# Two iterations a unit in place of three in the attention stream of a perceiver kernel

## Chip, core and metric

The kernel runs as one program on one core of a Trainium2 chip. The metric is the time of an execution on the device in microseconds (us), median over several runs. The engines are named as in the profile: PE is TensorE (matmuls), PEld its weight loads, DVE VectorE, ACT ScalarE, POOL GpSimd, and SP the queue that issues nearly all DMAs. Each engine takes its instructions in the order in which the program lists them.

## The reference

The model is a perceiver of two layers: cross attention, self attention and a feed-forward block, twice, each added to the stream `x`. Most of the time goes into the two cross attentions, of 64 queries per batch entry against a context of 1601 rows, for 32 entries and 16 heads of 16 values:

```python
x   : (32, 64, 256)      ctx : (32, 1601, 256)
# layer 0 (layer 1 is alike, with a mask over the context and no output projection)
q = split_heads(layernorm(x) @ wq + bq)
k = split_heads(ctx @ wk + bk)
v = split_heads(ctx @ wv + bv)
p = softmax(q @ k.T [+ mask], axis=-1)
x = x + concat(p @ v) @ wo + bo
```

The self attentions and feed-forward blocks of layer 0 are computed beside this stream, the last two blocks of layer 1 after it.

## The kernel before

`stream()` computes both cross attentions. Its work is cut into 256 **units** `u`: 2 layers x 32 batch entries x 4 groups of four heads. For a unit the kernel does the following, all in an order that is written out by hand (the framework places the waits, not the order):

- `maxima(u)` (L1225): scores with queries on the partitions, for the row maxima alone. Four steps of four matmuls `sp` (L1236, on 64x64 corners of the array) and two DVE reductions `mx` (L1241) each; the fourth step also makes the negated maximum `neg`, `mm`. A fifth step turns it with four small matmuls `rp` (L1256, one output row each) and copies it on ACT into a row of the query tile `qst` (two copies, L1261), so that the score matmuls that follow subtract it.
- `probabilities(u, j)` (L1267) for j = 0 to 6: scores with the context on the partitions, matmuls `tp` (L1277, whole array; 8 for each j, 4 for j = 6) into one of two PSUM buffers of `ps_t`, and one ACT exponential `e` (L1282) into one of three buffers of the pool `pt`.
- `weighted(u, j, e)` (L1285): the sums of values weighted by `e`, matmuls `acc` (L1292, on 32-column strips of the array).

Keys and values are made 1.8 batch entries ahead by the generator `projections()` (L1069). It alternates between a **keys call** (12 matmuls `kp`, L1089, and two DVE copies `kr` with the bias, L1095) and a **values call** (12 matmuls `vp`, L1117, and one ACT copy `v` out of PSUM, L1122, right behind them). A pair of context blocks needs one of each, and a unit needs 3.25 calls. `keys_values(target, slack)` (L1300) makes as many as its target asks for.

Each pair of blocks also needs casts on ACT, which are held as generators in the list `cuts` and moved on by `tick()` (L1005): `chi` (L986; POOL makes `clo` from it) splits a loaded block for the matmuls, and `ks` (L1039 and, when POOL has taken the difference, L1046) splits keys into three parts, which a DMA then stores to `kd` (L1049). A tick runs at most `left = 2` such pieces of work, and issues the loads `raw` (L974) that were listed one tick earlier (`loads`, then `due`). `fetch(u + 2)` (L1187) reads a unit's keys back with eight DMAs on SP (L1203 and L1208, a ninth with the mask in layer 1) into one of three `kst` buffers; the buffer is free when the last `tp` matmuls of unit u - 1 have read it.

PSUM buffers of `ps_m` (five, handed out in turn by `bank`) hold `sp`, `kp`, `vp`, `rp` and what the side work needs. The **side work** (queries, self attention and feed-forward of layer 0, the ends of finished rows) is moved on by `group_step()` and `end_step()`, one step at a call; its tiles lie in the pool `bg` by tags.

Before, a unit has three iterations. On PE their order is:

```
i=0: sp sp | acc(u-1: 5,6)        | tp 0,1 | side work | projections | tp 2
i=1: sp sp | acc(u: 0,1,2)        | tp 3,4 | side work | projections |
i=2:         acc(u: 3,4) | rp(u+1)| tp 5,6 | side work | projections | side work
```

with a tick before each of the three projections.

Of the kernel before, what the change touches and what calls it, by code (L numbers as in the profile page):

```python
# [20 lines left out]
F32 = mybir.dt.float32  # L21
# [9 lines left out]
P = 128  # L31
# [15 lines left out]
NH = 32  # L47
# [14 lines left out]
class Kernel:  # L62
# [215 lines left out]
    def stream_setup(self, wp, bg, bank):  # L278

        nc, ins = self.nc, self.ins  # L280
# [36 lines left out]
        yield  # L317
        self.eye = wp.tile([P, NQ], BF16, tag="eye", name="eye")
        nc.vector.tensor_tensor(self.eye, self.ident[:, :64], self.ident[:, 64:], ALU.add)
        tri = bg.tile([P, P], F32, tag="oT", name="tri")  # L320
        nc.gpsimd.memset(tri, 1.0)
        nc.gpsimd.affine_select(
            out=tri, in_=tri, pattern=[[-1, P]], compare_op=ALU.is_gt, fill=0.0,
# [185 lines left out]
    def stream(self):  # L509
        nc, tc, ins = self.nc, self.tc, self.ins  # L510
        with ExitStack() as ctx:
# [6 lines left out]
            kq = pool("kq")  # L518
            kp_ = pool("kst")
            vp_ = pool("v")  # L520
            pt = pool("pt", 3)
            small = pool("s", 4)
            work = pool("w", 2)
            bg = pool("bg", 1)
# [281 lines left out]
            def self0(g):  # L806
                xT = yield from normed(g, "sa0")
                rp = bank(f"sa0_rp{g}")
                for cc in range(2):
                    nc.tensor.matmul(  # L810
                        rp[: 3 * NH, : 2 * P], self.basT[:, cc, : 3 * NH], xT[:, cc, :],
                        start=(cc == 0), stop=(cc == 1),
                    )
                rT = bg.tile([3 * NH, 2 * P], F32, tag="oT", name=f"sa0_rT{g}")
                nc.scalar.copy(rT, rp[: 3 * NH, : 2 * P])
                yield
                qp = bank(f"sa0_qp{g}").rearrange("p (c n) -> p c n", c=2)
                for c in range(2):
                    nc.tensor.matmul(
                        qp[:, c, :], self.wT[:NH, c * P : (c + 1) * P], rT[:NH],  # L820
                        start=True, stop=True,
                    )
                qT = bg.tile([P, 2, 2 * P], F32, tag="qf", name=f"sa0_qT{g}")
                nc.scalar.mul(qT, qp, 0.25)
                yield
                kp = bank(f"sa0_kp{g}").rearrange("p (c n) -> p c n", c=2)
                for c in range(2):
                    nc.tensor.matmul(
                        kp[:, c, :], self.wT[NH : 2 * NH, c * P : (c + 1) * P], rT[NH : 2 * NH],
                        start=True, stop=True,  # L830
                    )
                kT = bg.tile([P, 2, 2 * P], F32, tag="kT", name=f"sa0_kT{g}")
                nc.scalar.copy(kT, kp)
                yield
                values(g, "sa0", [rT[2 * NH : 3 * NH]], [self.wT[2 * NH : 3 * NH]], None)
                yield

                def out(t, oT):
                    rp = bank(f"sa0_ro{g}_{t}")
                    for c in range(2):  # L840
                        nc.tensor.matmul(
                            rp[:NH, :P], self.basT[:, c, 3 * NH :], oT[:, c, :],
                            start=(c == 0), stop=(c == 1),
                        )
                    ro = bg.tile([NH, P], F32, tag="ro", name=f"sa0_rs{g}_{t}")
                    nc.scalar.copy(ro, rp[:NH, :P])
                    yield
                    ao = bank(f"sa0_ao{g}_{t}")
                    nc.tensor.matmul(ao[:, :D], ro, self.woT, start=True, stop=True)
                    x = self.X[:, 2 * g + t, :]  # L850
                    nc.vector.tensor_tensor(x, x, ao[:, :D], ALU.add)
                    yield

                yield from attention(g, "sa0", qT, kT, None, out)

            def ffn0(g):
# [12 lines left out]

                def wide(tag, dt=F32):  # L870

                    home = dict(dg="oT", row="ro").get(tag, f"ff_{tag}")
                    return bg.tile([P, 2, NQ], dt, tag=home, name=f"ff0_{tag}{g}")


# [113 lines left out]
                )  # L989
                return hi, lo  # L990

            kds, vs, ksts, cuts, loads, due = {}, {}, {}, [], [], []

            vring = [
                [
# [9 lines left out]
            def tick(b=-1):  # L1005


                if b < 0:
                    due[:], rest = loads[:], due[:]
                    del loads[:]  # L1010
                    for one in rest:
                        one()
                left = 2
                for one in list(cuts):
                    work = one[1] == "work"
                    if one[0] > b and work:
                        if left == 0:
                            continue
                        left -= 1
                    while True:  # L1020
                        one[1] = next(one[2], None)
                        if one[1] is None:
                            cuts.remove(one)
                        if one[1] is None or one[0] > b:
                            break
# [6 lines left out]
            def parted(i, x, quick):  # L1032

                m = 2 * width(i)
                ks = work.tile([P, 3, 2, KG], BF16, tag="ks", name=f"ks{i}", bufs=3)
                eng = nc.vector if quick else nc.gpsimd
                yield "work"
                x = x[:, :, :m]
                nc.scalar.copy(ks[:, 0, :, :m], x)  # L1039
                eng.tensor_tensor(x, x, ks[:, 0, :, :m], ALU.subtract)  # L1040
                eng.tensor_tensor(ks[:, 2, :, :m], x, upper(x), ALU.subtract)  # L1041
                if not quick:

                    yield "wait"
                    yield "work"
                nc.scalar.copy(ks[:, 1, :, :m], upper(x))  # L1046
                yield "store"
                for b, k0, n, o in spans(i):
                    nc.sync.dma_start(  # L1049
                        kds[b].rearrange("s (c q) (h n) -> (q h) s c n", c=2, h=4)[  # L1050
                            :, :, :, k0 : k0 + n
                        ],
                        ks[:, :, :, o : o + n],
                    )
# [10 lines left out]
            keyed = {}  # L1065

            NEVER = 2 * NB

            def projections():  # L1069

# [32 lines left out]
                def values(i):  # L1103
# [8 lines left out]
                    for i1 in range(2):  # L1112
                        o = slice(i1 * w_, (i1 + 1) * w_)
                        j = 0
                        for cc in range(2):
                            for x, w in ((hi, 0), (hi, 1), (lo, 0)):
# [2 lines left out]
                                    start=(j == 0), stop=(j == 5),  # L1119
                                )  # L1120
                                j += 1
                    nc.scalar.copy(  # L1122
                        v[:w_, :, :, :16], vp[:w_].rearrange("p c (h d) -> p c h d", d=16)
                    )
                    return 12 * D

                def fetched(i):
# [19 lines left out]

                def halved(i):
                    if raws[i] is None:
                        left = due + loads  # L1150
                        del due[:], loads[:]
                        for one in left:
                            one()
                    parts[i] = split(i)
                    return
                    yield
# [30 lines left out]
            def fetch(u):  # L1187

                b, q4 = divmod(u, 4)
                while keyed.get(b, 0) < NCH:  # L1190
                    made[0] += next(proj)
                tick(b)
                k = kring[u % 3]
                if u == 2:
# [197 lines left out]
            def banks_made(n):  # L1392
                for _ in range(n):
                    made[0] += next(proj)
                    tick()

            banks_made(1)
# [11 lines left out]
            fetch(1)  # L1409
            banks_made(3)  # L1410
            LEAD = 1.8
            for i, _ in enumerate(maxima(0)):
                if i < 4:
                    banks_made(1)
            groups.append((15, self.stream_setup(wp, bg, bank)))
            late = []
            for u in range(NU):
# [14 lines left out]
                    groups.append((u + 15, queries(*divmod((u + 15) // 16, NG))))  # L1432
                if u + 2 < NU and u + 2 not in ksts:
                    fetch(u + 2)
                nat = maxima(u + 1) if u + 1 < NU else iter(())

                for i, js in enumerate(((0, 1, 2), (3, 4), (5, 6))):
                    for _ in range((2, 2, 0)[i]):
                        next(nat, None)
                    for done in late:  # L1440
                        weighted(*done)
                        if done[1] == 6 and done[0] % 8 == 7:
                            n, t = divmod(done[0] // 8, NT)
                            ends.append((n, t, finish(n, t)))
                            next(ends[-1][2])
                    if i == 2:
                        next(nat, None)
                    late = [(u, j, probabilities(u, j)) for j in js[:2]]
                    banks[0] = 0
                    group_step()  # L1450
                    end_step()
                    tick()
                    keys_values(LEAD + (3 * u + i + 1) / 12.0, 0.15)
                    late += [(u, j, probabilities(u, j)) for j in js[2:]]
                    if i == 2:
                        group_step()
                        if u % 2:
                            end_step()
                for _ in nat:
                    pass  # L1460
            for done in late:
                weighted(*done)
            ends.append((1, NT - 1, finish(1, NT - 1)))
# [973 lines left out]
```

## Time and profile before

| what | value |
|---|---|
| time, median of 3 runs | 3648.9 us (3648.11 to 3666.66) |
| the profiled execution, and its span | 3643.7 us, 3642.0 us |
| granted TensorE clock over the span | 0.956 (0.98 to 1.00 from 300 to 3050 us, 0.83 after 3150 us) |
| last `acc` of the stream | at about 3108 us |
| from 300 to 3000 us: PE, PEld, DVE, ACT, POOL busy | 2591, 2171, 1735, 1885, 1468 us of 2700 |
| one exponential `e` (L1282) | 565 ns mean, 1792 of them |
| one cast `chi` (L986), `ks` (L1039, L1046) | 609, 606, 610 ns |
| one copy `v` out of PSUM (L1122) | 588 ns, 416 of them |
| one copy of the maxima (L1261) | 364 ns, two a unit |
| one bias copy `kr` on DVE (L1095) | 470 ns, two a keys call |
| one `clo` on POOL (L987) | 1246 ns |
| DMAs that read keys back (L1203, L1208) | 1024 of 208 KB and 1024 of 104 KB |
| DMA engines busy in the stream | 0.73 to 0.85 of the time, 200 to 240 GB/s |

Busy times are unions of what one engine has in flight. A matmul's recorded duration (195 to 305 ns) is its latency; matmuls follow one another much closer than that, so a PE that is busy all the time may still be slowed at the places where its starts lie further apart. For those, starts in the timeline are read.

### The profile page before, as it was taken

The numbers are of one execution on the slowest core, as the hardware profiler recorded it, in microseconds if no ns is written. First come the engines' busy times: TensorE is split into PE (matmuls) and PEld (weight loads), VectorE is DVE, ScalarE is ACT, GpSimd is POOL, SyncE is SP. The second block draws the span as 40 slices with busy tenths as digits, with TensorE's granted clock in tenths as the row PEclk, the third lists the DMA queues.
The fourth block names the chain that finished last, engine by engine and source line by source line (L and its number), as shares of the span: only waits on it lengthen the run. The fifth ranks groups of instructions, "written<-read, shape, count | busy, mean of one in ns | idle before, by whom it ended". The sixth has DMA issues, their size and how long they took to land. (4 is left out here: it accounts for less than half of the span.)

```text
span 3642.0 us, 148306 instructions
## 1 busy us (share of the span) xinstructions
PE 3316.4 (91%) x62993; PEld 2707.7 (74%) x63007; DVE 2417.2 (66%) x6166; ACT 2367.8 (65%) x4656; POOL 1792.4 (49%) x2109
## 2 busy tenths in 40 slices
PE   6899999999999999999999999999999998775698
PEld 5678887878778787778887778878778786332467
DVE  4556665666666566566667666656666566789879
ACT  3677766767667776667676777677667676154562
POOL 2455454555545554545555655556456563003246
PEclk8999999999999999999999999999999999887699
DMA  7888777777777777777787777777778887100000
GB/s 179 214 231 230 203 191 213 205 207 201 204 193 205 211 208 214 200 198 200 204 216 210 199 209 197 195 210 202 206 206 232 231 241 194 60 1 1 1 5 20
DMA packets 616920, 651.22 MB, mean 179 GB/s; under 512 B 127216, under 2 KB 581444, under 8 KB 599684
## 3 DMA queue, kind: packets, MB, share of 16 engines
q1 hardware_dynamic: 616256, 641.73, 64.3%
q8 instruction: 495, 8.11, 1.0%
q14 instruction: 169, 1.38, 0.1%
HBM read 468.30 MB, written 171.11 MB: 176 GB/s over the span
## 5 line engine op out<-in xcount | busy, mean ns | idle before, releaser
L1241 DVE TENSOR_REDUCE mx<-sp 128x1 f32<-128x400 f32 (+1 forms) x2048 | 1031.8, 565 | 324.5 <-PE sp L1236 323.9
L1282 ACT ACTIVATE e<-tp 128x512 f32<-128x512 f32 (+1 forms) x1792 | 931.7, 565 | 465.4 <-PE tp L1277 456.4
L987 POOL TENSOR_TENSOR clo<-raw,chi 128x512 fp32r<-128x512 f32 (+1 forms) x408 | 508.3, 1246 | 558.7 <-ACT chi L986 552.4
L1040 POOL TENSOR_TENSOR kr<-kr,ks 128x512 f32<-128x512 f32 (+1 forms) x406 | 459.4, 1132 | 608.7 <-ACT ks L1039 570.9
L1095 DVE TENSOR_SCALAR kr<-kp,bk 128x256 f32<-128x256 f32 (+1 forms) x832 | 356.3, 470 | 542.1 <-PE kp L1089 441.0
L1277 PE MATMUL tp<-qst,kst 128*128 128x64 bf16 (+1 forms) x13312 | 579.9, 195 | 15.0 <-ACT e L1282 13.1
L1292 PEld LDWEIGHTS acc<-e,v 128*17 128x17 f32 x26624 | 395.6, 98 | 213.2 <-issue 139.7
L1292 PE MATMUL acc<-e,v 128*17 128x64 f32 x26624 | 540.9, 222 | 13.2 <-ACT e L1282 10.5
L1277 PEld LDWEIGHTS <-kst 128*128 128x128 bf16 (+1 forms) x13312 | 462.2, 100 | 114.8 <-issue 22.0
L1117 PE MATMUL vp<-w_hi,chi 128*128 128x256 f32 (+1 forms) x1664 | 508.0, 305 | 15.7 <-DVE w_hi L222 12.4
L1117 PE MATMUL vp<-w_lo,chi 128*128 128x256 f32 (+1 forms) x1664 | 473.3, 284 | 0.4 <-DVE w_lo L223 0.3
L1117 PE MATMUL vp<-w_hi,clo 128*128 128x256 f32 (+1 forms) x1664 | 473.6, 285 | 0.0
L1041 POOL TENSOR_TENSOR ks<-kr 128x512 bf16<-128x512 f32 (+1 forms) x406 | 413.5, 1018 | 31.9
L1236 PE MATMUL sp<-kst,qst 64*64 64x400 bf16 (+1 forms) x4096 | 319.2, 349 | 92.0 <-DMA kst<-kd 41.2
L1089 PE MATMUL kp<-chi,w_hi 128*128 128x256 f32 (+1 forms) x1664 | 371.3, 305 | 14.4 <-DVE w_hi L222 6.2
L1122 ACT COPY v<-vp 128x512 f32<-128x512 f32 (+1 forms) x416 | 244.8, 588 | 184.9 <-PE vp L1117 181.7
L1089 PE MATMUL kp<-clo,w_hi 128*128 128x256 f32 (+1 forms) x1664 | 339.0, 285 | 15.3 <-POOL clo L987 14.5
L1117 PEld LDWEIGHTS vp<-w_hi,chi 128*128 128x128 f32 (+1 forms) x1664 | 313.9, 189 | 33.5 <-issue 9.5
L1089 PE MATMUL kp<-chi,w_lo 128*128 128x256 f32 (+1 forms) x1664 | 337.4, 285 | 0.0
L986 ACT CAST chi<-raw 128x512 fp32r<-128x512 f32 (+1 forms) x410 | 249.8, 609 | 105.6 <-DMA raw<-in_ctx_dram 105.4
L1117 PEld LDWEIGHTS vp<-w_lo,chi 128*128 128x128 f32 (+1 forms) x1664 | 314.6, 189 | 1.7 <-DVE w_lo L223 0.9
L1117 PEld LDWEIGHTS vp<-w_hi,clo 128*128 128x128 f32 (+1 forms) x1664 | 313.7, 189 | 0.0
(721 smaller groups left out, 5113.0 us busy)
## 6 DMA issues: line engine op xcount, KB each, us to landing
kst<-kd SPq DMA_DIRECT2D x1024, 208.0 KB
kd<-ks SPq DMA_DIRECT2D x384, 384.0 KB
kst<-kd SPq DMA_DIRECT2D x1024, 104.0 KB
raw<-in_ctx_dram SPq DMA_DIRECT2D x379, 256.0 KB
qst<-xa_qd SPq DMA_DIRECT2D x192, 64.0 KB
kd<-ks SPq DMA_DIRECT2D x64, 108.0 KB
xa_qd<-xa_qs SPq DMA_DIRECT2D x16, 384.0 KB
raw<-in_ctx_dram SPq DMA_DIRECT2D x62, 72.0 KB
```

The lines of the kernel that those rows point to most:

```text
L986: nc.scalar.copy(hi[:, :, :n], raw[:, :, :n])
L987: (nc.vector if i < 2 else nc.gpsimd).tensor_tensor(lo[:, :, :n], raw[:, :, :n], hi[:, :, :n].bitcast(F32), ALU.subtract)
L1040: eng.tensor_tensor(x, x, ks[:, 0, :, :m], ALU.subtract)
L1041: eng.tensor_tensor(ks[:, 2, :, :m], x, upper(x), ALU.subtract)
L1089: nc.tensor.matmul(kp[:, oc, :m], wk[w][:, cc, oc * P : (oc + 1) * P], x[:, cc, :m], start=(j == 0), stop=(j == 5),)
L1095: nc.vector.tensor_scalar(r[:, oc, :m], kp[:, oc, :m], self.bk[n][:, oc : oc + 1], None, ALU.add,)
L1117: nc.tensor.matmul(vp[:w_, i1, :], x[:, cc, o], wv[w][:, cc, :], start=(j == 0), stop=(j == 5),)
L1236: nc.tensor.matmul(sp[a][64 * j : 64 * j + 64, :n], q[r, h0 + 2 * j + a, tok], k[r, 2 * a + j, k0 : k0 + n], start=True, stop=True,)
L1241: nc.vector.tensor_reduce(mx[:, a, g : g + 1], sp[a][:, :n], AX.X, ALU.max)
L1277: nc.tensor.matmul(sp[:m, c, h, :], k[:, 2 * (h % 2) + h // 2, k0 : k0 + m], q[:, h0 + h, tok], start=True, stop=True,)
L1282: nc.scalar.activation(e[:m, :two], sp[:m, :two], AF.Exp)
L1292: nc.tensor.matmul(acc[32 * h : 32 * h + 17, slot, :], vs[b, c][:m, 4 * q4 + h, :], e[:m, c - 2 * i, h, :], start=(c == 0), stop=(c == NCH ...
```

## The change

A unit has two iterations. The order on PE becomes:

```
i=0: sp sp | acc(u-1: 4,5,6) | rp(u) | side work | projections | tp 0,1 | side work | projections | tp 2,3
i=1: sp sp | acc(u: 0,1,2,3) | side work | tp 4,5 | projections | tp 6 | side work
```

A tick stands behind each of the two `acc`, and runs up to three pieces of work. The fifth step of `maxima(u)` (`rp` and the two copies) moves from the end of unit u - 1 to the first iteration of unit u, behind the tick. A values call's copy `v` is listed in `held` and given to ACT later, by `copied()`: in front of the next projections and at the end of an iteration. Loads are issued by the first tick behind their listing (`due` is gone); the second cast of `ks` comes one tick behind the first, not two. `banks`, which limits the projections, no longer counts the side work. `end_step` is called four times a unit, not three or four. `pt` has four buffers, for which five tiles of `bg` take other tags.

```diff
-        tri = bg.tile([P, P], F32, tag="oT", name="tri")
+        tri = bg.tile([P, P], F32, tag="e", name="tri")
...
-            pt = pool("pt", 3)
+            pt = pool("pt", 4)
...
-                rT = bg.tile([3 * NH, 2 * P], F32, tag="oT", name=f"sa0_rT{g}")
+                rT = bg.tile([3 * NH, 2 * P], F32, tag="kz", name=f"sa0_rT{g}")
...
-                    ro = bg.tile([NH, P], F32, tag="ro", name=f"sa0_rs{g}_{t}")
+                    ro = bg.tile([NH, P], F32, tag="xT", name=f"sa0_rs{g}_{t}")
...
-                    home = dict(dg="oT", row="ro").get(tag, f"ff_{tag}")
+                    home = dict(dg="kz", row="kT").get(tag, f"ff_{tag}")
...
                 if b < 0:
-                    due[:], rest = loads[:], due[:]
+                    now = loads[:]
                     del loads[:]
-                    for one in rest:
+                    for one in now:
                         one()
-                left = 2
+                left = 3
...
                 eng.tensor_tensor(ks[:, 2, :, :m], x, upper(x), ALU.subtract)
-                if not quick:
-
-                    yield "wait"
-                    yield "work"
+                yield "work"
                 nc.scalar.copy(ks[:, 1, :, :m], upper(x))
...
+            def copied():
+
+                for one in held:
+                    one()
+                del held[:]
...
-                    nc.scalar.copy(
+
+                    held.append(lambda: nc.scalar.copy(
                         v[:w_, :, :, :16], vp[:w_].rearrange("p c (h d) -> p c h d", d=16)
-                    )
+                    ))
...
-                nat = maxima(u + 1) if u + 1 < NU else iter(())
-
-                for i, js in enumerate(((0, 1, 2), (3, 4), (5, 6))):
-                    for _ in range((2, 2, 0)[i]):
+                nat, own = maxima(u + 1) if u + 1 < NU else iter(()), nat
+
+                def some(*js):
+                    late.extend((u, j, probabilities(u, j)) for j in js)
+
+                def behind():
+
+                    group_step()
+                    end_step()
+
+                def made_up_to(part):
+                    copied()
+                    banks[0] = 0
+                    keys_values(LEAD + (u + part) / 4.0, 0.15)
+
+
+                for i in range(2):
+                    for _ in range(2):
                         next(nat, None)
                     for done in late:
                         weighted(*done)
...
-                    if i == 2:
-                        next(nat, None)
-                    late = [(u, j, probabilities(u, j)) for j in js[:2]]
-                    banks[0] = 0
-                    group_step()
-                    end_step()
+                    late = []
                     tick()
-                    keys_values(LEAD + (3 * u + i + 1) / 12.0, 0.15)
-                    late += [(u, j, probabilities(u, j)) for j in js[2:]]
-                    if i == 2:
-                        group_step()
-                        if u % 2:
-                            end_step()
-                for _ in nat:
-                    pass
+                    if i == 0:
+                        next(own)
+                        behind()
+                        made_up_to(1 / 3.25)
+                        some(0, 1)
+                        behind()
+                        made_up_to(2 / 3.25)
+                        some(2, 3)
+                    else:
+                        behind()
+                        some(4, 5)
+                        made_up_to(1.0)
+                        some(6)
+                        behind()
+                    copied()
```

The start of the program calls `copied()` behind each projection call too, so nothing changes there but the ticks.

## Prediction

> **What bounds the kernel now.** I read the page first: engine totals, then the slices.
>
> ```profile
> PE 3316.4 (91%) x62993; PEld 2707.7 (74%) x63007; DVE 2417.2 (66%) x6166; ACT 2367.8 (65%) x4656; POOL 1792.4 (49%) x2109
> PE   6899999999999999999999999999999998775698
> ```
>
> PE is above nine tenths from slice 3 to 34, the stream (to about 3108 us). What follows it, some 530 us, the change does not touch. Next, sums over single units late in the stream, where there is no side work (columns: stretch, its length, then busy us of PE, PEld, DVE, ACT, POOL, clock, DMA share, GB/s):
>
> ```profile
> 2914.60:2923.80 9.20, 9.20 (x213) 7.90 (x212) 5.32 (x13) 7.86 (x17) 5.57 (x6) 1.00 0.65 168
> 2933.00:2943.70 10.70, 10.70 (x229) 9.36 (x229) 6.19 (x15) 7.49 (x16) 5.97 (x6) 1.00 0.88 244
> ```
>
> Three projection calls make a unit of 9.2 us, four one of 10.7, and PE is busy for all of both, ACT for 70 to 85%. So a unit is as long as PE's own order, and ACT has 1.3 to 3.2 us to spare. Then the waits from 300 to 3000 us, 228 units (total us, times, longest):
>
> ```profile
> PE sp L1236 <- DMA kst<-kd: 13.9, 14, 3.3
> PE tp L1277 <- ACT e L1282: 8.5, 8, 1.7
> PE acc L1292 <- ACT e L1282: 3.9, 3, 3.0
> PE sp L1236 <- ACT v L1122: 1.1, 4, 0.4
> ...
> ACT e L1282 <- PE tp L1277: 394.1, 431, 5.2
> ACT chi L986 <- DMA raw<-in_ctx_dram: 70.4, 29, 5.5
> ...
> SPq L1203 <- PE tp L1277: 190.1, 109, 7.1
> ```
>
> PE hardly waits for ACT; ACT waits for PE. What the order of PE can save must therefore lie between matmuls. The timeline of the unit at 2933 us shows it (start, length, engine, line):
>
> ```profile
> 2933.00 0.54 PE L1236 MATMUL sp<-kst,qst 64*64 64x401 bf16 x8
> 2933.10 0.58 ACT L1122 COPY v<-vp 72x512 f32<-72x512 f32 x1
> ...
> 2933.46 0.53 PE L1292 MATMUL acc<-e,v 128*17 128x64 f32 x24
> ...
> 2933.59 0.62 ACT L986 CAST chi<-raw 128x512 fp32r<-128x512 f32 x1
> ...
> 2933.93 0.64 PE L1277 MATMUL tp<-qst,kst 128*128 128x64 bf16 x16
> ...
> 2935.93 0.41 PE L1277 MATMUL tp<-qst,kst 128*128 128x64 bf16 x8
> ...
> 2936.26 0.54 PE L1236 MATMUL sp<-kst,qst 64*64 64x400 bf16 x8
> ...
> 2936.73 0.86 PE L1292 MATMUL acc<-e,v 128*17 128x64 f32 x48
> ...
> 2937.53 0.64 PE L1277 MATMUL tp<-qst,kst 128*128 128x64 bf16 x16
> ...
> 2939.39 0.28 PE L1117 MATMUL vp<-w_hi,clo 128*128 128x256 f32 x1
> ...
> 2939.60 0.64 PE L1292 MATMUL acc<-e,v 128*17 128x64 f32 x32
> ...
> 2940.07 0.29 PE L1256 MATMUL rp<-identb,mm 128*1 128x128 bf16 x4
> 2940.28 0.54 PE L1277 MATMUL tp<-qst,kst 128*128 128x64 bf16 x12
> 2940.39 0.74 ACT L1261 CAST qst<-rp 1x256 bf16<-1x256 f32 x2
> ```
>
> From start to start: 24 `acc` until `tp` take 0.47 us, 48 take 0.80, so one takes 13.75 ns and leaving `acc` for the whole array costs 0.47 - 0.33 = **0.14 us**. The last `vp` is followed by `acc` after 0.21, where one `vp` follows another after 0.12: entering costs **0.09**. Eight `tp` until `sp` take 0.33, at 29 ns each (16 in 0.47): 0.09 for that change. Between `tp` and projections, both on the whole array, nothing is lost.
>
> **The change, part by part.**
>
> *Fewer changes of shape on PE.* Before, a unit leaves or enters a shape eight times: sp-acc twice, acc-tp twice, tp-sp, projections-acc, rp-tp, projections-sp. After: sp-acc twice, rp-projections, tp-sp twice, acc-tp; six. Projections-sp becomes tp-sp (0.09 both), rp-tp becomes rp-projections (taken as equal: both go to the whole array). One projections-acc and one acc-tp go: 0.09 + 0.14 = 0.23 us a unit. About 250 units have projections, so 0.23 x 250 = **-58 us**. No matmul goes. Bounds: 0, if another wait takes its place, to -70 (0.14 for both).
> The Trainium skill (TensorEngine Tiling (Array Packing), Key Properties) says that changing the tiling mode drains TensorE, without a price; TensorE: Matmul & The Clock Gate, Part 2, has a drain of some 128 cycles, 53 ns at 2.4 GHz, by which two changes fewer are an estimated 27 us. The rows show about twice that, and the sum uses the rows.
>
> *Exponentials.* `acc` 0 to 2 now follow `tp` 2 closely; after, they have the same two `sp` steps before them, but no copy `v` in front of their `e`. Of 8.5 + 3.9 us of waits I take **-8** (0 to -12).
>
> *ACT in front of tp 0.* The copies of the maxima lay some 3.4 us (median over units 20 to 249, from their end to the start of `tp` 0 in the trace) ahead of their reader; now the tick's casts stand before them and one projection call behind. Two ACT instructions in a row overlap by 0.09 (2933.10 + 0.58 against 2933.59), so a cast takes 0.52 net, `v` 0.50. From the last `tp` 6 matmul, without side work: PE needs 0.12 + 0.46 (sp) + 0.59 (40 acc) + 0.21 (rp) + 1.53 (12 kp from 2934.40 to 2935.93) = 2.91. ACT ends `e` 6 after 0.27 + 0.37 = 0.64, continues from 0.55, then takes one cast (before: a values call, so + `v`) or three (before: a keys call), and 0.74 for the copies: 0.55 + 0.50 + 0.52 + 0.74 = 2.31, or 0.55 + 1.56 + 0.74 = 2.85; both in time. Behind a double call (one unit in four) there are `v` and three casts: 3.35 + 0.06, late by 0.5. Side work lies in that stretch twice, and adds more to PE (by the trace's starts 1.45 us a unit, mean over its four places) than to ACT (0.81). A quarter of the units have none: 60/4 x 0.5 = 8 us; of the other 190, a quarter has about 0.2 to spare, and half of these wait some 0.3: 7 us. With 5 for single keys calls, **+20** (0 to +110, which is a wait of 0.5 in nine units of ten). Behind tp 3, `e` 4 must be done for tp 6: 1.17 + three casts 1.56 + 0.60 = 3.33 against 0.09 + 0.46 + 0.88 + 0.14 + 0.47 + 1.53 = 3.57 on PE; no wait, and up to 0.3 in few units, which lies in those bounds.
> A rule that speaks against the change: TensorE: Matmul & The Clock Gate (on queue depths) has ScalarE strictly in order, so a `chi` that waits for its load holds up the copies and tp 0; if half of the 70.4 us of such waits came through, 35 us would be added, and 5 of the 40 saved below would be left.
>
> *Reading keys back.* tp 6 of u - 1, which frees `kst`, comes behind the last projections, about 2 us later (1.53 and side work). In 109 of 228 units SP waits for it. From the end of the eighth issue (L1208) to the `sp` that needs it the trace has 8.1 us in the median unit, under 2.9 in a tenth, 0.8 at least. Most hide 2 us; the tight units are held by SP's queue, not by this release. **+4** (0 to +50).
>
> *Held copies.* A `v` behind two `e` keeps its PSUM buffer 1 us longer. Now 1.1 us of waits; **+2** (-1 to +12).
>
> *At nothing:* loads a tick earlier and stores (as many issues, SP has room behind the fetch; -6 to +6); the first ten pairs' second cast a tick later (the start waits for DMA; +-3); `end_step` four times; the fourth `pt` buffer; five tags, whose former tiles are read steps before (+-3); the last six units without projections, 8 us each, where copies and exponentials show (-8 to +8).
>
> Sum: -58 - 8 + 20 + 4 + 2 = **-40 us**: 3643.7 - 40 = 3603.7 for such an execution, and 3648.9 - 40 = **3609 us** for the median, which lies 5 us above the profiled one.
>
> **Rivals.** *ACT becomes the gate in front of tp 0.* For: three casts at 62% of first ticks (of four units three end with one call, half of them keys, and one with two: 2.5 of 4), each able to wait for a load, DVE or POOL; the room of 3.4 us is given up. Against: ACT idles 394 us behind tp now. Price: 0.6 us in 62% of 250 units = 94 in place of 20: 3609 + 74 = 3683. It decides from a mean wait of 0.24 us a unit ((58 + 8 - 6)/250), where the gain is gone.
> *The saving is taken up* at the next bank, `clo` or side step: for it, side work fills three units in four and has waits of its own; against, units without it are PE throughout. 3642.
> *SP is late:* if the tenth of units with under 2.9 us waits 2 us each, 25 x 2 = 50 less the 4: 3655. Against: such units are gated by the queue.
>
> **Numbers.** A measurement tells 0.5%, 18 us, from no change. Forecast 0.58, its own range 3585 to 3633 (ACT from 0 to 45); taken up 0.17; ACT 0.19; SP 0.06. The ACT and SP cases are slower or nearly so; faster 0.58, within 0.5% 0.19, slower 0.23. The range reaches down to 3583 (no ACT wait) and up to 3672, which leaves out half of the ACT case.
>
> **What would show it.** Right: units without side work and with three calls at about 9.0 us; two runs of `acc` a unit; ACT waiting for tp less than 394 us; `PE tp <- ACT qst` a short row. Wrong: PE waiting for L1261's copies or `e` by over 60 us in all, ACT's share in such units near 90% with PE starts further apart; `sp <- DMA kst` well over 40 us; side-work units no shorter while the others are.

## The result, and the profile after

The changed kernel took 3902.73 us (median of 4 runs, 3891.99 to 3908.88) where the kernel before took 3648.53 on the same chip: a ratio of **1.068** [1.064, 1.072] (in brackets, here and below, the 95% interval). It is slower by 254 us, against a forecast of 40 us faster. The profiled execution is the one of 3891.99 us. Its engine totals, busy slices and granted clock, and two groups (busy and mean ns; idle before):

```profile
PE 3353.9 (86%) x63007; PEld 2784.7 (72%) x63007; DVE 2579.8 (66%) x6166; ACT 2368.2 (61%) x4656; POOL 1796.8 (46%) x2109
...
PE   6798998989989999898898889888888888684688
...
PEclk8999999999999999999899999999999999796689
...
L1282 PE MATMUL tp<-qst,kst 128*128 128x64 bf16 (+1 forms) x13312 | 586.3, 196 | 191.7 <-ACT qst L1266 166.6
...
L1043 ACT COPY ks<-kr 128x512 bf16<-128x512 bf16 (+1 forms) x416 | 252.1, 606 | 197.7 <-POOL kr L1040 194.6
```

ACT and POOL are busy for the same time as before, PE for 38 us more, and DVE for 163 us more although it runs the same instructions. PE's row of nines has become a row of eights and nines: the stream has holes now. The last weighted sums start 248 us later than before (3355.7 against 3107.8 us), and the 535 us behind them are unchanged, so all of it was lost in the stream. The waits from 300 to 3000 us, as shown of before:

```profile
ACT e L1287 <- PE tp L1282: 630.1, 605, 4.5
...
ACT ks L1043 <- POOL kr L1040: 162.5, 127, 4.1
PE tp L1282 <- ACT qst L1266: 125.5, 98, 4.1
...
PE sp L1241 <- ACT v L1126: 9.3, 19, 0.8
...
PE tp L1282 <- ACT e L1287: 8.6, 16, 1.4
...
PE sp L1241 <- DMA kst<-kd: 7.5, 8, 2.2
```

Two rows are all but new (before, ACT waits at most 2 us for POOL at that cast, and no tp waits for the copies) and belong together: ACT's second key cast (L1043) waits for POOL's difference, and PE's tp 0 waits for the copies of the maxima (L1266), which stand behind that cast on ACT. ACT waits *more* for PE than before (630 against 394 us), not less. A unit with three projection calls and no side work, 9.20 us before, is now

```profile
3135.46:3147.30 11.84, 9.43 (x216) 8.16 (x213) 6.25 (x13) 7.52 (x15) 6.16 (x6) 1.00 0.81 227
```

and its timeline, from the end of the unit before to tp 0, says why (start, length; in brackets the engine's idle time before it and what ended that):

```profile
3136.38 0.62 ACT L1043 COPY ks<-kr 128x512 bf16<-128x512 bf16 x1
...
3136.53 0.28 PE L1261 MATMUL rp<-identb,mm 128*1 128x128 bf16 x4
...
3136.90 0.62 ACT L1039 CAST ks<-kr 128x512 bf16<-128x512 f32 x1
...
3137.42 0.62 ACT L986 CAST chi<-raw 128x512 fp32r<-128x512 f32 x1
...
3137.60 1.17 POOL L1040 TENSOR_TENSOR kr<-kr,ks 128x512 f32<-128x512 f32 x1 [1.62 <-ACT ks L1039]
...
3138.79 0.62 ACT L1043 COPY ks<-kr 128x512 bf16<-128x512 bf16 x1 [0.75 <-POOL kr L1040]
...
3139.44 0.74 ACT L1266 CAST qst<-rp 1x256 bf16<-1x256 f32 x2
...
3140.23 0.63 PE L1282 MATMUL tp<-qst,kst 128*128 128x64 bf16 x16 [1.80 <-ACT qst L1266]
```

`fetch(u + 2)` opens a unit and has a `tick(b)` of its own, which also moves later batches' casts on. So two ticks stand in a row at the unit's start: the fetch's (the second cast of the pair before at 3136.38, then L1039, `chi`) and the first iteration's (L1043). Between them ACT has nothing to do. The second cast of the *same* pair could start 1.14 us after the first did (3138.04, behind `chi`), but needs POOL's 1.17 us, which begin only when the first is done: it waits 0.75. The copies, ready since the end of rp at 3136.81, start at 3139.44, and tp 0 behind them. Before, the step "wait" put a tick between the two casts, and the copies had been done 3.3 us (median) ahead of tp 0. After, that median is 0.05 us, and in 141 of 232 units tp 0 starts within 0.15 us of the copies' end.

To size this I summed PE's time over units 16 to 247 in each trace: idle PE; the half lost of what ran in stretches granted half clock; and the rest, matmuls at full clock (waits shorter than a matmul's 0.2 to 0.35 us hide in it).

| us | before | after | a_woi | x_own | x_rpt |
|---|---|---|---|---|---|
| length | 2766.8 | 3004.2 | 2885.1 | 2845.4 | 2795.3 |
| idle PE | 111 | 313 | 220 | 134 | 132 |
| lost to clock | 35 | 95 | 88 | 44 | 52 |
| matmuls at full clock | 2621 | 2596 | 2577 | 2667 | 2612 |
| idle at tp 0 | 0 | 149 | 22 | 0 | 0 |
| at side work | 11 | 44 | 59 | 13 | 18 |
| at rp | 5 | 26 | 25 | 0 | 2 |
| at the first maxima (keys read back) | 39 | 18 | 46 | 49 | 67 |
| at the fourth of the maxima's eight banks | 6 | 29 | 9 | 28 | 0 |

(The last three columns are experiments.) The matmuls did become 25 us shorter, as the change means; 202 us of idle time and 60 us of lower clock were paid for it.

### The profile page after: what moved, and what is told of

It reads as the page before. It is cut to its first block, busy times and chain, and to the rows that moved or that the text cites. A ratio compares the mean times of both kernels' runs of the same rounds, so it can differ in the third digit from the quotient of the medians.

```text
span 3890.3 us, 148268 instructions
## 1 busy us (share of the span) xinstructions
PE 3353.9 (86%) x63007; PEld 2784.7 (72%) x63007; DVE 2579.8 (66%) x6166; ACT 2368.2 (61%) x4656; POOL 1796.8 (46%) x2109
## 5 line engine op out<-in xcount | busy, mean ns | idle before, releaser
L1282 PEld LDWEIGHTS <-kst 128*128 128x128 bf16 (+1 forms) x13312 | 509.6, 101 | 263.7 <-issue 221.1
L1297 PE MATMUL acc<-e,v 128*17 128x64 f32 x26624 | 491.3, 225 | 1.7 <-issue 1.5
L1241 PE MATMUL sp<-kst,qst 64*64 64x400 bf16 (+1 forms) x4096 | 336.8, 353 | 78.0 <-DMA kst<-kd 24.9
L1043 ACT COPY ks<-kr 128x512 bf16<-128x512 bf16 (+1 forms) x416 | 252.1, 606 | 197.7 <-POOL kr L1040 194.6
L1092 PEld LDWEIGHTS kp<-chi,w_hi 128*128 128x128 f32 x1664 | 264.1, 196 | 49.8 <-DVE mx L1246 20.4
```

The lines of the kernel that those rows point to most:

```text
L1092: nc.tensor.matmul(kp[:, oc, :m], wk[w][:, cc, oc * P : (oc + 1) * P], x[:, cc, :m], start=(j == 0), stop=(j == 5),)
L1241: nc.tensor.matmul(sp[a][64 * j : 64 * j + 64, :n], q[r, h0 + 2 * j + a, tok], k[r, 2 * a + j, k0 : k0 + n], start=True, stop=True,)
L1282: nc.tensor.matmul(sp[:m, c, h, :], k[:, 2 * (h % 2) + h // 2, k0 : k0 + m], q[:, h0 + h, tok], start=True, stop=True,)
L1297: nc.tensor.matmul(acc[32 * h : 32 * h + 17, slot, :], vs[b, c][:m, 4 * q4 + h, :], e[:m, c - 2 * i, h, :], start=(c == 0), stop=(c == NCH ...
```

## Experiments

Theory A: the wait for POOL between two casts in a row, ahead of the copies and tp 0, makes the loss. Rival B: the mere number of casts ahead of the copies does. Rival C: the values, held back, give up their PSUM buffers too late. Later theories (D, E, T, B5, H) are named where they are first tested. "The third pair of the maxima's banks" in some expectations is the fourth bank of a unit.

All times are medians; ratios are to the kernel before, run on the same chip in the same job. Differences between runs of different jobs are of medians; by the ratios they come within 8 us of that. Rows of waits and sums of waits in this section are from 300 to 3150 us, idle times by place from units 16 to 247. "After" is the changed kernel, and each diff is against it unless it says otherwise.

**1. The wait for POOL, taken away in three ways.** a_wait puts the step between the casts back:

```diff
+                if not quick:
+                    yield "wait"
                 yield "work"
                 nc.scalar.copy(ks[:, 1, :, :m], upper(x))
```

> The changed kernel with the tick of waiting between the two casts of ks put back (two ticks between them in place of one). Theory A (the second cast L1043 stands on ACT right behind the first, because the tick inside fetch and the first tick of the unit have nothing between them; it waits there for POOL's difference, and the copies of the maxima and tp 0 wait behind it): ACT's waits for POOL at the second cast fall from 198 us to under 40, the excess in front of tp 0 from 171 us to under 70, time 3750 to 3800. Rival B (the mere number of casts in front of the copies): the second casts stay in front of the copies of some unit, time 3860 to 3900. Rival C (values held back, so that PSUM buffers come free late): no change, 3880 to 3910.

3817.44 us, **1.045** [1.038, 1.051]: 85 us come back, 17 less than theory A's range asks for and 43 more than rival B's allows. ACT's idle time in front of the second cast falls from 198 to 4 us in the whole run; tp 0 still idles 39 us.

a_flush lets the fetch's tick touch only its own batch (`tick`: `if one[0] > b >= 0: continue`), so that the two ticks no longer come in a row.

> The changed kernel with the tick inside fetch confined to what that fetch needs, so that a unit really has two ticks. Theory A: half a unit lies between the two casts, as with the waiting tick; waits for POOL under 40 us, time 3740 to 3800. Rival B: at most three casts, not up to six, stand in front of the copies; also faster, but the waits for POOL that remain do not matter: 3780 to 3850. Rival C: 3880 to 3910.

3884.72 us, 1.063 [1.057, 1.069]: a miss. The idle time in front of the second cast goes to 5 us here too, but with two ticks a unit the chain of a pair is too slow, and new waits take its place:

```profile
ACT ks L1041 <- DMA kd<-ks: 149.2, 56, 7.5
PE tp L1284 <- ACT e L1289: 81.7, 52, 6.2
```

The first cast waits for a buffer whose store has not landed, and the exponentials behind it make tp 6 late (78 us of idle PE). Taking the fetch's tick away from later pairs is no cure; section 3 moves ticks instead.

a_own issues rp and the copies ahead of the tick instead:

```diff
                     late = []
+                    if i == 0:
+                        next(own)
                     tick()
                     if i == 0:
-                        next(own)
                         behind()
```

> The changed kernel with rp and the copies of the maxima ahead of the first tick's casts instead of behind them. Theories A and B: the copies wait only for the casts of the tick inside fetch; the excess in front of tp 0 falls from 171 us to under 50; the exponentials 0 and 1 now stand behind the second cast, so that by A some 198 us of ACT's waits for POOL remain and come out at tp 2 in part: 3740 to 3820. By B the same without a wait at tp 2: 3700 to 3750. Rival C: over 3850.

3780.54 us, **1.034** [1.029, 1.040]: 122 us come back. tp 0's idle time falls from 149 to 16 us. This edit also takes the copies from behind the casts themselves, so that the 37 us over a_wait can be rival B's part; no run tells the two apart. a_wait_own does both.

> Both edits, the waiting tick and the copies ahead of the casts. Theory A: nothing of the two losses is left, and the saving of two changes of shape a unit (58 us predicted) shows against before: 3600 to 3680. Rival C (PSUM buffers late): 60 to 100 us of it remain: 3700 to 3760.

3795.58 us, 1.039 [1.033, 1.044], no better than a_own alone, and outside the ranges of both theories. ACT waits 59 us for POOL in a_own and next to nothing here, which gains no time: with the copies ahead of the casts this wait no longer reaches PE. So the two cures are for the same loss and do not add: it is worth 85 to 125 of the 254 us, and something else costs the rest.

The step alone, in the old order, is b_nowait (the kernel before without its `yield "wait"`):

> The kernel before, with nothing changed but that the step between the two key casts is left out. In the old order the fetch's tick and the unit's first tick have two exponentials, 16 maxima and 24 to 40 weighted sums between them, and the copies of the maxima are done by then. Theory A: ACT waits for POOL under 60 us, PE hardly waits behind it, 3640 to 3675. Rival: leaving the step out costs what it costs in the new order, where putting it back gained 85 us: 3700 to 3740.

3718.09 us, **1.018** [1.015, 1.021]; the rival was right. The copies of the maxima do not stand behind the casts there, but exponentials do:

```profile
PE acc L1291 <- ACT e L1281: 48.5, 49, 3.9
PE tp L1276 <- ACT e L1281: 26.9, 28, 3.1
```

ACT waits 120 us for POOL, and PE 75 us for exponentials, against 23 in the kernel before. So the missing step is a loss in the old order too, at another place.

**2. The copies back at the unit's end, and the held values.** a_back_wait moves rp and the copies behind tp 6 of the unit before and puts the step back; a_back has no step; a_bwi is a_back_wait with `nc.scalar.copy(v...)` run at once in place of `held.append(lambda: ...)`.

```diff
-                nat, own = maxima(u + 1) if u + 1 < NU else iter(()), nat
+                nat = maxima(u + 1) if u + 1 < NU else iter(())
...
-                        next(own)
...
                         some(6)
+                        next(nat, None)
```

> After, with the row maxima's transposition and its two copies (rp, qst) back at the end of the unit before, behind tp 6, and with the step between the two key casts back. State of the account so far, from the traces, units 16 to 248: after lost 202 us of idle PE and 60 us of slower clock against before, and gained 25 in matmuls; with rp and copies merely ahead of the tick (a_own) 111 and 49 are left. Theory A (the seam: copies behind casts, and rp and the next projection bank directly behind the four banks of the maxima, so that they wait for DVE's reductions): waits at tp 0 gone, at rp 0 under 8 us (25 in a_own), at the first projection under 6 (12 in a_own); time 3640 to 3710. Theory D (two thirds of the loss is the two-iteration order itself: group steps and the fifth to eighth bank of the maxima crowd each other wherever rp stands): time 3740 to 3790.

> As a_back_wait, without the step between the two key casts (as the changed kernel has it). Theory A': the second cast still waits for POOL right behind the first (ACT's wait for POOL's difference 130 us or more, as after), but with the copies done a unit ahead only the exponential of tp 0 stands behind it, and that has a projection call to hide it: within 25 us of a_back_wait. Theory D': each wait of ACT for POOL comes through wherever the copies stand: 60 us or more above a_back_wait, as after stands 85 above a_wait.

> As a_back_wait, with the values copied out of PSUM at once, not held behind the exponentials. Theory C (held values keep a bank too long): the waits at the third pair of maxima's banks for the values' copy (9.6 us in a_own by the waits view) go, 10 to 25 us faster than a_back_wait. Rival: the copy lies in front of an exponential that PE needs next, as before had it: PE's waits for e rise by 5 to 15 us, and the time is equal within 10 us.

3849.2 us, 1.053 [1.050, 1.057]; 3831.24, 1.048 [1.045, 1.052]; 3780.78, **1.035** [1.032, 1.038]. Theories A and D both missed a_back_wait: tp 0 no longer waits, and it is slower than a_own by 69 us. a_back's ACT waits 167 us for POOL and it costs nothing above a_back_wait: with the copies out of the way that wait is covered. And the values copied at once gain 68 us, far over theory C's 25. The waits of a_back_wait:

```profile
PE sp L1243 <- DVE kr L1100: 38.8, 35, 3.2
PE sp L1243 <- ACT qst L1268: 37.2, 82, 0.7
PE rp L1263 <- DVE mm L1257: 29.5, 58, 0.7
```

The maxima wait for whoever reads the PSUM buffer that comes round next: a held value keeps one of the five for the length of two exponentials, and rp one until its copies. In a_bwi the second row is 5.3 us, and the idle time at the third and fourth of the maxima's eight banks falls from 98 to 43 us.

a_woi asks the same of the change's own order: a_wait_own with the values copied at once.

> After with three things put back or moved: the step between the two key casts back, the unit's rp and copies of the maxima ahead of the tick, and the values copied out of PSUM at once. Beside a_wait_own (3796) only the last differs. Theory C (held values keep a bank or a place in ACT's order too long, as the 68 us between a_bwi and a_back_wait show): 3745 to 3780, and waits of sp for the values' copy gone. Rival (there it was the copy waiting behind the copies of the maxima at the unit's end, which here do not stand there): within 10 us of 3796.

3770.27 us, **1.034** [1.031, 1.037]; against a_wait_own 0.5%, some 17 us by the ratios, whose intervals overlap. The time lies in C's range, but a gain this small is not shown beyond doubt; that it is smaller than in a_bwi because rp does not stand in the same stretch is a guess.

**3. The place of the ticks.** a_woi_t is a_woi with the second iteration's `tick()` behind `some(4, 5)`; b_tick is the kernel before with the change's ticks (`left = 3`, loads not put off through `due`).

> As a_woi, with the tick of the second iteration behind the matmuls of tp 4 and 5 (where before had its ticks) in place of behind the weighted sums. Theory E (the tick there sets POOL's differences beside DVE's two small casts of the maxima, 0.2 us each before and 0.5 us after, and DVE's queue then holds up rp, the group steps and the banks): the two casts fall from some 240 us in all to under 150, group-step and rp waits from some 80 us to under 50, 30 to 70 us faster than a_woi. Theory D (the order alone crowds the banks): casts and time within 15 us of a_woi.

> The kernel before, with the ticks of the change alone: up to three later batches' entries step in one tick in place of two, and loads are issued at the next tick and not the one behind it. The prediction put these at nothing: 3635 to 3665. Rival: with three entries in a tick the casts and their POOL differences pile up in the old order too: ACT waiting for POOL over 40 us, 3680 to 3720.

b_tick: 3642.2 us, 0.998 [0.996, 1.000], nothing, as predicted. a_woi_t: 3769.19, 1.034 [1.031, 1.037]. Theory E's causes came as expected; the time is theory D's, no other than a_woi's. DVE's work on `mm`, from 300 to 3000 us, is 86.6 us before, 193.8 after, 219.2 in a_woi and 72.7 in a_woi_t; the idle time at side work, at rp and at the projection behind rp falls from 113 to 49 us. But it comes back elsewhere: a_woi_t's projections now wait for `clo` (26 us by the waits), its weighted sums of pair 6 for their exponential (28 us) and tp 0 for the copies (41 us; on ACT, ahead of them, the first key cast waits 86 us for stores to land, 66 in a_woi). The stall moved to other results of ACT and POOL.

x_own and x_back move all of it. x_own has rp and the copies at the very start of the unit, ahead of the fetch; the ticks behind tp 0 and 1 and behind tp 4 and 5; values copied at once; no step between the casts. x_back is a_bwi with its ticks behind tp 0 and 1 and behind tp 6.

```diff
+                next(nat)
                 if u + 2 < NU and u + 2 not in ksts:
                     fetch(u + 2)
...
-                    tick()
...
                         some(0, 1)
+                        tick()
...
                         some(4, 5)
+                        tick()
```

> Two iterations a unit with the key casts' ticks where the kernel before had them, behind exponentials (behind tp 0 and 1, and behind tp 4 and 5; the third is the fetch's), the unit's rp and copies of the maxima at its very start ahead of the fetch, the values copied at once, and no step between the two key casts. Theory T (what remains after the copies are cured is the ticks' place: the casts, POOL's differences and clo crowd ACT, POOL and DVE at the unit's seam): idle PE from 220 to under 150 us, time 3680 to 3730. Theory D (two iterations leave less room between the maxima's banks, projections and group steps, wherever the ticks are): 3750 to 3790, with waits only moved.

> As a_bwi (rp and copies behind tp 6, step between the casts, values copied at once; 3781), with the first tick behind tp 0 and 1 and the second behind tp 6 and the copies. Theory T: the two small casts of the maxima on DVE fall from 260 us to under 130 in all, rp's wait for them (31 us) goes, 3690 to 3740. Theory D: within 20 us of 3781.

x_own: 3727.95 us, **1.022** [1.018, 1.026], the upper end of theory T; idle PE falls to 134 us and the clock's loss to 44. ACT waits just 18 us for POOL, though the step is missing. Several things differ from after at once, and no run says what each is worth in this order. x_back: 4017.84, 1.103 [1.098, 1.108], a miss of both theories by over 200 us. Its second tick stands directly ahead of the fetch's, so again two come in a row, and with the one behind tp 1 all three lie ahead of the exponentials of pairs 2 and 3: PE waits 54.5 us for these in acc, and the gaps inside acc are 68 us longer in all than in x_own. That is a quarter of the 290 us between the two; what makes the rest was not found.

**4. One PSUM buffer fewer a unit.** In x_own the gaps between matmuls of the maxima are still 65 us longer than before, and its waits name readers of the shared buffers. The next edit takes rp out of that rotation:

```diff
-                rp = bank(f"rp{u}")
+                rp = ps_t.tile([P, 512], F32, tag="tp", name=f"rp{u}")
```

applied to a_woi, to x_own (x_rpt) and to the kernel before (b_rpt).

> As a_woi (3770), with rp in a buffer of the scores' PSUM pool (tp) and not in one of the five banks that maxima, rp, projections and group steps share. Theory B5 (in two iterations the eight banks of the maxima, rp and the projections come round too fast for five, so that rp 0, the first projection matmul and the third pair of maxima wait for DVE's and ACT's readers: 54 us of idle in a_woi): rp 0's wait under 6 us, the projections' under 10, 3710 to 3745. Rival (DVE and ACT are late whatever the bank, and the wait goes to the next reader): 3755 to 3785.

> As x_own (3728), with rp in the scores' pool as in a_woi_rpt. Theory B5: in x_own the gaps from maxima matmul to maxima matmul are 65 us longer than before, and PE waits for the copies (10 us) and for DVE's kr (14 us), whose banks come round: 20 to 55 us of it go, 3670 to 3710. Rival: within 15 us of 3728.

> The kernel before, with rp in the scores' pool. Theory B5: three iterations leave the banks time (waits at maxima 2 and 3 and at the projections by DVE or ACT under 15 us in the whole stream), so at most 10 us can be gained, and tp 5 and 6, which need the same pool right behind rp, can lose some: 3635 to 3665.

a_woi_rpt: 3731.09 us, 1.022 [1.020, 1.025]; x_rpt: 3667.76, **1.004** [1.002, 1.005]; b_rpt: 3748.97, 1.026 [1.024, 1.028]. The same line gains 39 and 60 us in the two orders of two iterations, as theory B5 has it (x_rpt is 2 us faster than its range), and loses 95 in the order of three, where 3635 to 3665 was expected: a miss. x_own, then x_rpt:

```profile
PE sp L1241 <- DMA kst<-rows: 27.6, 14, 5.0
PE sp L1241 <- DMA kst<-kd: 23.2, 20, 3.7
PE sp L1241 <- DVE kr L1098: 14.1, 36, 1.5
...
PE sp L1241 <- ACT qst L1266: 10.4, 28, 0.5
```

```profile
PE sp L1241 <- DMA kst<-kd: 34.1, 22, 5.2
PE sp L1241 <- DMA kst<-rows: 32.4, 15, 5.0
PE tp L1282 <- ACT e L1287: 16.8, 34, 0.8
```

The rows for DVE and for the copies are gone. In the old order rp's new buffer is one that tp needs at once, which the expectation named and priced far too low:

```profile
PE tp L1277 <- ACT qst L1261: 126.6, 230, 2.3
```

So for two iterations theory B5 holds: the maxima, rp and the projections follow each other, and with one buffer fewer asked for, the idle time at the maxima's fourth bank goes from 28 us to none. With three iterations, matmuls of tp lie between the maxima and the next user of a buffer; that five are enough there was not tested apart, since b_rpt loses at tp.

x_rpt_h gives x_rpt the held copies back (it is then after with only the ticks, rp and rp's buffer moved):

> The changed kernel with four lines moved and its held value copies kept: rp in the scores' PSUM pool, rp and the copies at the unit's very start ahead of the fetch, the ticks behind tp 0 and 1 and behind tp 4 and 5. Beside x_rpt (3668) only the values' copies differ, which here follow the exponentials. In x_rpt PE loses some 40 us inside the weighted sums of pairs 2 and 3, whose exponentials stand behind casts and a values copy. Theory H (the held copies do what they are for once a bank is free): 15 to 40 us less, 3630 to 3655, about the kernel before or a little faster. Rival (as in a_back_wait and a_wait_own, a held value keeps its bank too long for the third pair of maxima): 3665 to 3710.

3689.85 us, 1.011 [1.008, 1.013]. Theory H's range is missed and the rival's holds, but both effects are there: the gaps inside acc shrink by 36 us, as the held copy is for, those inside the maxima grow by 60 (`sp <- ACT v`: 15.1 us in 40 waits), and the sum is a loss.

No version beat the kernel before (b_tick can't be told from it). Of the last 14 us in x_rpt the trace puts 28 at the keys read back (idle at the first maxima 67 against 39 us) and some 40 at the sums of pairs 2 and 3 (starts of acc further apart than before), against the gains in shape. That is read from its trace; no run took these two away.

## Why the prediction was wrong

**The step that failed** is *ACT in front of tp 0*, +20 (0 to +110). Its place was right and its price was not: PE idles there for 149 us in 232 units. The casts were priced by their busy time, with two ticks a unit. The fetch's tick was left out, though the unit's `fetch` calls it, and with it the fact that a pair's two casts now run back to back with POOL's 1.17 us between them. The working had at most `v` and three casts in front of the copies, done 3.35 us after the last tp 6 matmul. In the unit above there are `v` and four (3.87 by the same prices), and 0.75 of waiting: 4.8 us after it (`e` 6 ends at 3136.01, 0.67 behind that matmul's start; the copies end at 3140.18). The lower end of the range does not follow from the terms either: 3609 less the 20 of this step is 3589, not 3585 or 3583.

**"At nothing"** listed "the first ten pairs' second cast a tick later" and not the other 406, whose second cast comes a tick *earlier* because the step "wait" is gone. That part alone costs 67 us in the old order (b_nowait) and 85 in the new (a_wait), though nothing once the copies are out of its way (a_back, a_own). The same paragraph gave the order of the PSUM buffers no term at all; one buffer a unit is worth 39 to 60 us there. The loads and the three pieces of work in a tick, also at nothing, were right in the old order (b_tick).

**Fewer changes of shape, -58.** The count and the prices hold in the trace. The order has nine changes before and seven after, not eight and six, since the list leaves out acc to rp on both sides; the difference of two stands. In units 16 to 247 projections hand over to acc 217 times before and never after, and acc hands over to tp or side work 464 times before and 236 after; such an exit takes 0.154 us from start to start before and 0.14 to 0.16 after, where one acc takes 0.015. At the means of before, 0.08 for an entry and 0.139 for an exit, that is an estimated 49 us, where the term is 53 for these units. Matmuls at full clock are only 25 us shorter in after (44 in a_woi); waits too short to show as idle time count as matmul time there, and no figure here splits the two. x_rpt saves less: its 464 exits from acc to tp, projections or side work all remain (0.15 to 0.18 each), and what vanishes is acc to rp at 0.061, with the 217 entries some 28 us.

**Exponentials, -8.** `acc <- e` (3.9 us) is gone, `tp <- e` is 8.6 us after 8.5: half of it.

**Reading keys back, +4 (0 to +50).** Hidden behind larger waits in after (18 us of idle time against 39). With those removed it shows: +28 in x_rpt, inside the bounds.

**Held copies, +2 (-1 to +12).** In after the row `sp <- ACT v` is 9.3 us, within its bounds. What copying at once gains is outside them: 22 us net (x_rpt_h against x_rpt) and 68 beside rp (a_bwi); the 17 of a_woi are not clear of noise. The step gave the buffer 1 us more and did not ask who needs it next.

**The rivals.** "ACT becomes the gate" was the right story, down to casts that can wait for POOL; at 0.6 us in 62% of units it was priced at 94 us. The measured 0.64 us over *all* units make 149, and two costs stand outside it: 60 us of lower clock, and the buffers. Of the signs named, PE waiting for the copies of the maxima by over 60 us came (125.5); `sp <- DMA kst` well over 40 did not.

## What to carry to other kernels

When a step is taken out between two instructions on one in-order engine that are tied through another engine, count every place that steps the schedule (here the fetch's own tick), write down what then lies between the two, and price the second by the other engine's latency, not by its own length. When an order is made denser, count the shared buffers that are handed out between a buffer's writer and its reader: the matmuls that were moved away may have been what hid that reader. If one cure only moves the wait, move the whole group before concluding that the wait was not the cause.

## What the hardware showed unexpectedly

**A small DVE cast as long as a POOL operation.** The cast of 2 columns, `mm`, before and after (shortest, median, longest ns):

```profile
L1249 DVE CAST mm<-neg x256: 170/172/1159, 81.6 to 3098.2; 128x2 bf16<-128x2 f32 x128
```

```profile
L1254 DVE CAST mm<-neg x256: 171/625/1193, 81.3 to 3347.4; 128x2 bf16<-128x2 f32 x128
```

and one of them in after:

```profile
3144.77 1.04 POOL L1041 TENSOR_TENSOR ks<-kr 128x512 bf16<-128x512 f32 x1
...
3144.83 1.01 DVE L1254 CAST mm<-neg 128x2 bf16<-128x2 f32 x1
```

It starts 0.06 us behind POOL's operation and ends 0.03 us after it: 0.17 us of work become 1.01. The Trainium skill (SBUF — State Buffer, Who interferes with whom) says that DVE and GpSimd share one pair of ports as an exclusive lock, that a DVE cast or an operation with two SBUF inputs can need it, and that the one that comes second is blocked for the other's whole length; the row agrees.

**The clock drops after short gaps.** In units 16 to 247 the trace of after has 51 stretches of half clock (mostly 3.4 us long), the one before 19. The longest gap in the 7 us ahead of such a stretch is 1.9 us in the median (0.94 at least). Of 69 gaps over 1.5 us, 39 have a stretch begin inside them or within 4 us behind them; 6 us taken at random would hold such a start in one case of ten. The Trainium skill (TensorE: Matmul & The Clock Gate, HAM oscillation — how this bites in real kernels) gives idle gaps over some 3.4 us as the rule; here gaps of half that are enough in every second case. The loss goes with the long gaps and not with idle time as such:

| us | before | after | a_woi | x_own | x_rpt | b_rpt |
|---|---|---|---|---|---|---|
| idle PE | 111 | 313 | 220 | 134 | 132 | 199 |
| of it in gaps over 1.5 us | 55 | 145 | 119 | 52 | 67 | 37 |
| lost to clock | 35 | 95 | 88 | 44 | 52 | 22 |

b_rpt idles 88 us more than before, most of it in the 230 waits of half a us shown above, and loses less to the clock than before. That the gaps bring the clock down is read from these figures; no run changed them alone.
